# A convolution in Winograd-like form with four filtered positions: filter weights by accumulating transfers, shared rows copied, norm sums over eight rows, and the last reordering moved into the next chunk

## The chip, the cores and the metric

The kernel runs on one core of one Trainium2 chip. The metric is the device time of one execution in microseconds; the median of several runs counts. In the text, PE is TensorE, DVE is VectorE, ACT is ScalarE, POOL is GpSimd and SP is SyncE; PEld is PE's loading of weights.

## The reference, cut to what matters

Four layers work on x of shape (4, 256, 56, 56) in float32. Each normalises by groups of eight channels (`_gn`), applies a block and adds the result to its input.

```python
x = x + _L0_conv_ref(_gn(x), ...)   # involution, 7x7 window, weights computed from x
x = x + _L1_conv_ref(_gn(x), ...)   # residual block of two 3x3 convolutions
x = x + _L2_conv_ref(_gn(x), ...)   # involution with batch norms
x = x + _L3_conv_ref(_gn(x), ...)   # gates from the spectrum's mean and the channel mean

def _L1_conv_ref(x, w1, g1, b1, rm1, rv1, w2, g2, b2, rm2, rv2):
    h = _conv3x3(x, w1, stride=1)
    h = _bn(h, g1, b1, rm1, rv1)
    h = jax.nn.relu(h)
    h = _conv3x3(h, w2, stride=1)
    h = _bn(h, g2, b2, rm2, rv2)
    return jax.nn.relu(x + h)

def _gn(v, G=32, eps=1e-5):
    g = v.reshape(B_, G, C_ // G, H_, W_)
    m = jnp.mean(g, axis=(2, 3, 4), keepdims=True)
    s = jnp.var(g, axis=(2, 3, 4), keepdims=True)
    return ((g - m) / jnp.sqrt(s + eps)).reshape(v.shape)
```

The change concerns the second layer, `_L1_conv_ref`, alone.

## The kernel before, in words

`involution_layer` does layers 0 and 2 (the fourth layer's gates run inside its second call), and `conv_layer` the two 3x3 convolutions between them. Channels are two blocks of 128 partitions (`NB` = 2).

**The form.** Along a row, groups of four output pixels are computed from six transformed input values (positions k = 0 to 5) instead of by twelve products. `phases` normalises the loaded rows into four interleaved planes `ph1` on ACT (L1331). `transform` makes six position planes v from them in nine DVE instructions (L1355 to L1369); `input1` does so for the first convolution, `input2` for the second, out of `ph2`, in which the first leaves its result. For each position PE multiplies v with position weights (`unfiltered`, L1413: two input blocks times three row taps). In the first convolution, from chunk 1 on, the positions 1 to 4 (`K2`) are filtered along the rows too: `columns` (L1392 to L1395, DVE) combines rows of v, PE does four products (L1451) into an `inner` and an `outer` pair of PSUM banks, ACT copies one (L1461), and DVE joins them (L1465, L1466, L1468).

**The weights.** `u1_sb` and `u2_sb` hold six positions for each of two input blocks and three taps. `row_weights` loads positions 0 and 5 and computes positions 1 to 4 from the three filter columns on DVE, six instructions for each block (L1246 to L1255); `edge_weights` multiplies positions 0 and 5 on ACT (L1261). `column_weights` (DVE) and `filter_weights` (ACT, L1267) make the filtered weights of the first convolution.

**The order.** An image is three chunks of rows, so there are twelve chunks in each convolution: `C1_ROWS` is 20, 18, 18 rows and `C2_ROWS` is 16, 20, 20. The order on all engines is written out by hand: (1, 0), then (1, i), (2, i - 1) in turn, then (2, 11). Side work is put into twelve slots `after[0]` to `after[11]` of each chunk: `after[2 * n]` runs at the first half of the n-th position, `after[2 * n + 1]` behind it. `in_order` then ties each engine to this program order. In `conv1` the copy L1461 of a filtered position stands ahead of `after[2 * n]`.

**The end of a chunk.** `conv2` scales the residual (L1515, ACT), joins it with the result (L1527, DVE), reorders it by a relu on ACT (L1535), adds the layer's input by an accumulating DMA (L1536, POOL) and stores it (L1537, POOL). This is done for each half of the channels (`co` = 0, 1), at the chunk's end. In the next conv2 chunk `stats` takes the sums for the following norm, one instruction for each four rows (L1544). `conv1`'s last two outputs (L1430) are left in `tail1` and run in the following conv2 chunk; in the one place where a conv1 chunk follows another, chunk 1 after chunk 0, they run at its start.

**Buffers.** `mm_ps` has four tiles of two PSUM banks, which all the products take in turn, those of `norm_steps` too. `norm_steps` is a generator that advances at `after[5]` and `after[11]` and keeps its tile from the product (L217, L228) to the step in which DVE reads it (L220, L148). `y_tile(0)` to `y_tile(4)` and `y_tile(5)` are scratch for results. `v` has two buffers in turn.

Of the kernel before, what the change touches and what calls it, by code (L numbers as in the profile page):

```python
# [56 lines left out]
C2_ROWS = [(0, 16), (16, 36), (36, 56)]  # L57
ST_ROWS = 4

# [12 lines left out]
def net_kernel(  # L72
# [1109 lines left out]
    def conv_layer(xin, xout, st, ahead):  # L1182
        with ExitStack() as es:
# [44 lines left out]

            def row_weights(u, wc, raw=None):

                ws = []
                for ci in range(NB):
                    w = wc[ci * P : (ci + 1) * P].rearrange("c (y x) n -> c y x n", y=3)
                    nc.sync.dma_start(u[:, ci, :, 0, :], w[:, :, 0, :])
                    nc.sync.dma_start(u[:, ci, :, 5, :], w[:, :, 2, :])
                    us = [u[:, ci, :, k, :] for k in range(WPOS)]
                    if raw is None:
                        w1 = new_xr()[:, : 3 * C].rearrange("p (y n) -> p y n", y=3)
                        nc.scalar.dma_start(w1, w[:, :, 1, :])
                        ws.append((us[0], w1, us[5], *us[1:5]))  # L1240
                    else:
                        r = raw[ci][:, : 9 * C].rearrange("p (y x n) -> p x y n", y=3, x=3)
                        ws.append((r[:, 0], r[:, 1], r[:, 2], *us[1:5]))
                yield
                for w0, w1, w2, u1, u2, u3, u4 in ws:
                    tt(u2, w0, w2, ALU.add)  # L1246
                    tt(u1, u2, w1, ALU.add)
                    yield
                for w0, w1, w2, u1, u2, u3, u4 in ws:
                    tt(u2, u2, w1, ALU.subtract)  # L1250
                yield
                for w0, w1, w2, u1, u2, u3, u4 in ws:
                    stt(u4, w2, 4.0, w0, ALU.mult, ALU.add)
                    stt(u3, w1, 2.0, u4, ALU.mult, ALU.add)
                    stt(u4, w1, -2.0, u4, ALU.mult, ALU.add)  # L1255
                    yield

            def edge_weights(u, ci):

                for k, by in ((0, 6.0), (5, 24.0)):  # L1260
                    nc.scalar.mul(u[:, ci, :, k, :], u[:, ci, :, k, :], by)  # L1261

# [6 lines left out]
            def column_weights(ci, k0, k1):  # L1269

                w0, w1, w2 = (u1_sb[:, ci, y, k0:k1, :] for y in range(3))
                x = ux_sb[:, ci, k0 - 1 : k1 - 1, :]
                s = y_tile(3)[:, : (k1 - k0) * C].rearrange("p (k n) -> p k n", n=C)
                tt(s, w0, w2, ALU.add)
                tt(x, s, w1, ALU.subtract)
                tt(w1, s, w1, ALU.add)
# [38 lines left out]
            def phases(i):  # L1315

                y0, y1, lo, hi = rows1(i)
                n, r0 = y1 - y0 + 2, lo - (y0 - 1)
                rstd, shift = norms[1][i // 3]
                if y0 == 0:  # L1320
                    nc.vector.memset(ph1[:, :, 0], 0.0)
                if y1 == H:
                    nc.vector.memset(ph1[:, :, n - 1], 0.0)
                for ci in range(NB):
                    at = ci * (CV_ROWS + 2) * W
                    xr = room["rows"][:, at : at + (hi - lo) * W].rearrange("p (r t j) -> p j r t", t=WT, j=4)
                    for j in range(4):
                        q, t0 = (j + 1) % 4, (j + 1) // 4
                        dst = ph1[:, PL[q], r0 : r0 + hi - lo, ci, t0 : t0 + WT]
                        s, t = rstd[:, ci : ci + 1], shift[:, ci : ci + 1]  # L1330
                        nc.scalar.activation(dst, xr[:, j], AF.Identity, bias=t, scale=s)  # L1331
                        yield

            def transform(v, ph, y0, n):

                rows = ph[:, :, y0 : y0 + n].rearrange("p j r c t -> p j (r c) t")
                at, size = rows[:, 0:1], ph.shape[2] * NB * (WT + 1)
# [33 lines left out]

            def new_v(key):
                v_of[key] = work.tile([P, WPOS, (CV_ROWS + 2) * NB, WT], F32, name="v")
                return v_of[key]

            def input1(i):
                y0, y1, _, _ = rows1(i)
                n = y1 - y0 + 2
                yield from transform(new_v((1, i)), ph1, 0, n)

            def input2(i):
                y0, y1 = C2_ROWS[i % 3]
                yield from transform(new_v((2, i)), ph2, y0, y1 - y0 + 2)

# [32 lines left out]
            def conv1(i, after, tail):  # L1417
# [4 lines left out]
                a, t, b, s, q = (y_tile(k)[:, : NB * n * WT] for k in (0, 1, 2, 5, 4))  # L1422
                home = {1: q, 2: s, 3: t, 4: s, 0: s}

# [14 lines left out]
                for n_s, k in enumerate(KS):  # L1439
# [41 lines left out]
                    if k == 2:  # L1481
                        tt(full(a), full(q), got, ALU.add)
                        tt(full(q), got, full(q), ALU.subtract)
                    elif k == 4:
# [14 lines left out]
            def conv2(i, after, sums, tail):  # L1499
# [23 lines left out]
                def joined(co):  # L1523
# [7 lines left out]
                    if i == n_chunks - 1:  # L1531
                        stt(xj, rj, 0.0, xj, ALU.max, ALU.add)
                        nc.sync.dma_start(xout[bb][co][:, at], x)
                    else:
                        nc.scalar.activation(xj, rj, AF.Relu)  # L1535
                        nc.gpsimd.dma_start(x, xin[bb][co][:, at], accum_op=ALU.add)  # L1536
                        nc.gpsimd.dma_start(xout[bb][co][:, at], x)  # L1537

                def stats(co, ks):

                    x = xr_of[i, co]
                    for k in ks:
                        at = (k * ST_ROWS - y0) * W
                        nc.vector.bn_stats(sums[co][:, k, :], x[:, at : at + ST_ROWS * W])  # L1544

# [36 lines left out]

                ks = list(range(y0 // ST_ROWS, y1 // ST_ROWS))
                tail += [lambda co=co, part=part: stats(co, part) for co in range(NB) for part in (ks[:2], ks[2:])]


# [10 lines left out]
            order.append((2, n_chunks - 1))  # L1597
            late_v = None
            sums_of = {}


            since = mark()
            weights1, weights2 = row_weights(u1_sb, wc1, (room["h"], room["v2"])), row_weights(u2_sb, wc2)
            next(weights1)
# [24 lines left out]
            for s, (conv, i) in enumerate(order):  # L1629
                after = [[] for _ in range(12)]  # L1630
                for g in slow:
                    after[5].append(step(g))
                    after[11].append(step(g))
                nxt = order[s + 1] if s + 1 < len(order) else None
                if conv == 1:
                    run_all(tail1)

                    if nxt[0] == 2:
                        j = nxt[1]
                        late_v = input2(j)  # L1640
                        place(after, late_v, (1, 1, 3, 5, 8, 10))
                        if j == 0:
                            place(after, weights2, (3, 5, 7, 9, 11))
                        if i + 1 < n_chunks:
# [3 lines left out]
                    else:  # L1648
                        j = nxt[1]
                        place(after, phases(j), [k // 2 for k in range(8)])  # L1650
                        after[3].append(lambda: load_rows(j + 1, xin))
                        place(after, input1(j), [4 + k // 2 for k in range(9)])
                        for ci in range(NB):
                            after[2 + ci].append(lambda ci=ci: edge_weights(u1_sb, ci))
                            after[4 + ci].append(lambda ci=ci: column_weights(ci, 1, 3))
# [3 lines left out]
                        for ci in range(NB):  # L1659
                            after[9 + ci].append(lambda ci=ci: column_weights(ci, 3, 5))  # L1660
                            after[10 + ci].append(lambda ci=ci: filter_weights(ci, 3, 5))
                        after[11].append(step(weights2))
                    conv1(i, after, tail1)
                else:
                    if i % 3 == 0:
                        sums_of[i // 3] = [
                            new_sums(H // ST_ROWS, work, 4)
                            if i // 3 < B - 1
                            else small.tile([P, H // ST_ROWS, 6], F32, name=f"st_c{co}", bufs=1)
                            for co in range(NB)  # L1670
# [3 lines left out]
                    tail1 = []  # L1674
                    if i == 0:
                        for ci in range(NB):
                            after[ci].append(lambda ci=ci: edge_weights(u2_sb, ci))
                    if late_v is not None:
                        place(after, late_v, (0, 0, 1))
                        late_v = None  # L1680
                    stats_at, loads_at = ((1, 2, 3, 4), (2, 4)) if i < n_chunks - 1 else ((3, 4, 6, 7), (4, 7))
                    for at, f in zip(stats_at, tail2):
                        after[at].append(f)
                    tail2 = []
# [20 lines left out]

            return tail2, sums_of[B - 1]

# [77 lines left out]
```

## Time and profile before

| | |
|---|---|
| median of 3 runs | 1776.24 us (1775.5 to 1786.09) |
| the profiled execution | 1783.97 us |
| its span in the profile | 1782.2 us |
| PE busy | 1704.1 us (96%) |
| PE weight loads | 1504.1 us (84%) |
| DVE busy | 1333.3 us (75%) |
| ACT busy | 898.5 us (50%) |
| POOL busy | 397.1 us (22%) |

The profile shows one execution; its times count from the start of its span. A group of instructions is named by line, engine and tiles, with its count, its busy time and the idle time before it with what ended it. PEclk is the share of full clock that PE was granted. The convolutions' matmuls run from 520.3 to 1228.8 us, and a conv1 chunk begins there with L1451 rows and ends with L1413 rows.

### The profile page before, as it was taken

The numbers are of one execution on the slowest core, as the hardware profiler recorded it, in microseconds if no ns is written. First come the engines' busy times: TensorE is split into PE (matmuls) and PEld (weight loads), VectorE is DVE, ScalarE is ACT, GpSimd is POOL, SyncE is SP. The second block draws the span as 40 slices with busy tenths as digits, with TensorE's granted clock in tenths as the row PEclk, the third lists the DMA queues.
The fourth block names the chain that finished last, engine by engine and source line by source line (L and its number), as shares of the span: only waits on it lengthen the run. The fifth ranks groups of instructions, "written<-read, shape, count | busy, mean of one in ns | idle before, by whom it ended". The sixth has DMA issues, their size and how long they took to land.

```text
span 1782.2 us, 55628 instructions
## 1 busy us (share of the span) xinstructions
PE 1704.1 (96%) x24128; PEld 1504.1 (84%) x24128; DVE 1333.3 (75%) x2457; ACT 898.5 (50%) x1909; POOL 397.1 (22%) x591
## 2 busy tenths in 40 slices
PE   6999999999989999999999999998999999999898
PEld 4988988889978988898889889986888888888786
DVE  2777787767779887788778787865877677678675
ACT  2555556555554424432343334223667567577555
POOL 2224322333320000000000000001000554562572
PEclk9999999999999999999999999999999999999996
DMA  2445443633652123331333132233445666665643
GB/s 86 136 151 179 134 149 132 197 107 128 205 178 92 45 70 90 93 79 42 84 92 89 39 90 52 63 126 108 143 139 167 191 201 196 211 210 159 193 147 114
DMA packets 71074, 227.45 MB, mean 128 GB/s; under 512 B 13141, under 2 KB 20830, under 8 KB 67118
## 3 DMA queue, kind: packets, MB, share of 16 engines
q1 hardware_dynamic: 55038, 160.97, 28.6%
q0 software_dynamic: 13952, 60.87, 12.2%
q8 instruction: 190, 3.11, 0.7%
q10 hardware_dynamic: 1840, 2.05, 0.4%
q14 instruction: 54, 0.44, 0.1%
HBM read 88.00 MB, written 49.15 MB: 77 GB/s over the span
## 4 chain that ended last, share of the span: by engine, by line
PE 70%; DVE 17%; ACT 4%; issue 4%; DMA 3%; POOL 1%; SPq 1%; ACTq 0%; DVEq 0%; POOLq 0%
PE mm L1413 25%; PE ps L634 14%; PE ps L592 14%; PE mm L1451 7%; DVE kt L610 5%; PE ps L406 3%; DVE un L654 3%; DMA xw<-xw 2%; PE ps L468 2%; DVE st L1104 1%; DVE st L359 1%; ACT xs L1535 1%; ACT hp L487 1%; PE ps L717 1%; PE ps L946 1%
## 5 line engine op out<-in xcount | busy, mean ns | idle before, releaser
L1413 PE MATMUL mm<-v,u_sb 128*128 128x280 f32 (+2 forms) x2400 | 533.8, 384 | 1.2 <-DVE v L1367 1.2
L1413 PEld LDWEIGHTS mm<-v,u_sb 128*128 128x128 f32 x2400 | 452.4, 189 | 77.6 <-PE mm L1413 1.9
L634 PE MATMUL ps<-kt,xw 126*32 126x48 f32 (+1 forms) x12544 | 382.8, 236 | 31.2 <-issue 23.0
L634 PEld LDWEIGHTS ps<-kt,xw 126*32 126x32 f32 (+1 forms) x12544 | 343.2, 122 | 77.8 <-issue 55.5
L592 PE MATMUL ps<-hp,z_sb 64*126 64x133 f32 x6144 | 383.8, 279 | 7.3 <-DVE kt L610 4.4
L592 PEld LDWEIGHTS ps<-hp,z_sb 64*126 64x126 f32 x6144 | 365.0, 186 | 22.5 <-DVE kt L610 6.2
L610 DVE TENSOR_TENSOR kt<-ps,zb_sb 126x798 f32<-126x798 f32 x352 | 333.0, 980 | 60.2 <-PE ps L592 48.7
L603 ACT ACTIVATE kt<-ps,zb_sb 126x133 f32<-126x133 f32 x960 | 280.3, 441 | 105.8 <-PE ps L592 105.8
L654 DVE SCALAR_TENSOR_TENSOR un<-ps,s,un 128x240 f32<-128x240 f32 x224 | 102.4, 457 | 88.7 <-ACT un L649 84.5
L654 DVE SCALAR_TENSOR_TENSOR un<-ps,par_sb,un 128x240 f32<-128x240 f32 x224 | 97.9, 456 | 85.2 <-ACT un L647 81.2
L1451 PE MATMUL mm<-xs,u_sb 128*128 128x126 f32 (+1 forms) x1056 | 133.7, 280 | 7.7 <-DVE hp L1466 6.8
L1451 PEld LDWEIGHTS mm<-xs,u_sb 128*128 128x128 f32 x1056 | 127.9, 194 | 9.7 <-ACT ph L1331 8.3
L418 ACT COPY xw<-ps 126x896 f32<-126x896 f32 x112 | 101.3, 906 | 42.3 <-PE ps L406 22.4
L659 POOL TENSOR_TENSOR xs<-un,xs 128x240 f32<-128x240 f32 x112 | 72.2, 665 | 219.8 <-DVE un L654 219.8
L406 PE MATMUL ps<-ident_sb,strip_sb 128*126 128x128 f32 x784 | 112.7, 285 | 6.3 <-issue 3.0
L1536 POOL DMA_DIRECT2D xs<-x x22 | 19.7, 897 | 441.4 <-ACT xs L1535 441.4
L149 POOL TENSOR_TENSOR norm_sb<-norm_sb,mhalf 128x1 f32<-128x1 f32 x32 | 19.3, 605 | 432.6 <-DVE norm_sb L148 432.6
L647 ACT ACTIVATE un<-ps,par_sb 128x240 f32<-128x240 f32 x112 | 50.1, 448 | 122.5 <-PE ps L634 112.1
L649 ACT ACTIVATE un<-ps,bn_t,s 128x240 f32<-128x240 f32 x112 | 60.1, 537 | 98.5 <-PE ps L634 90.9
L1535 ACT ACTIVATE xs<-res 128x1120 f32<-128x1120 f32 (+1 forms) x22 | 45.9, 2088 | 126.6 <-DVE res L1527 126.6
L406 PEld LDWEIGHTS ps<-ident_sb,strip_sb 128*126 128x126 f32 x784 | 85.7, 143 | 17.4 <-POOL strip_sb L391 4.1
L1331 ACT ACTIVATE ph<-xs,norm_sb 128x294 f32<-128x294 f32 (+2 forms) x96 | 80.8, 896 | 8.8 <-DMA xs<-x 7.1
(253 smaller groups left out, 1819.8 us busy)
## 6 DMA issues: line engine op xcount, KB each, us to landing
xw<-xw SPq DMA_DIRECT2D x224, 252.0 KB
xw<-xw SPq DMA_DIRECT2D x224, 126.0 KB
xs<-x SPq DMA_DIRECT2D x24, 560.0 KB
x<-xs POOLq DMA_DIRECT2D x8, 1568.0 KB, 8.2
xs<-x SPq DMA_DIRECT2D x8, 1568.0 KB
xs<-in_x_dram SPq DMA_DIRECT2D x6, 1568.0 KB
x<-xs SPq DMA_DIRECT2D x6, 1568.0 KB
gx<-x POOLq DMA_DIRECT2D x42, 224.0 KB, 5.3
```

Of the source, the lines that this page charges most:

```text
L406: nc.tensor.transpose(ps[:Q, k * P : (k + 1) * P], flat[:, k * Q : (k + 1) * Q], ident_sb)
L418: nc.scalar.copy(xw[:, :NSB, :], ps[:Q, : NSB * P].rearrange("q (n c) -> q n c", n=NSB))
L592: nc.tensor.matmul(ps[:Q, i, k * NT : (k + 1) * NT], z_sb[i * R : (i + 1) * R, cb * GB // 2 + gp, z0 : z0 + Q], hp[i * R : (i + 1) * R, py ...
L603: nc.scalar.activation(kt[:, g0 + i, pb, :, k], ps[:Q, i, k * NT : (k + 1) * NT], AF.Identity, bias=zb_sb[:, cb * GB + g0 + i, p0 + k : p0 ...
L610: nc.vector.tensor_tensor(kt[:, g0 : g0 + 2, pb], ps[:Q, :, : PB * NT].rearrange("q i (k t) -> q i t k", k=PB), zb_sb[:, cb * GB + g0 : cb ...
L634: nc.tensor.matmul(v[m * j : m * j + m, i, :, k * TP : (k + 1) * TP], xw[:, window(ty), m * j : m * j + m], kt[:, ng * j : ng * j + ng, :, ...
L654: nc.vector.scalar_tensor_tensor(part, o[e], s, part, ALU.mult, ALU.add)
L659: nc.gpsimd.tensor_tensor(dst, u, dst, ALU.add)
L1331: nc.scalar.activation(dst, xr[:, j], AF.Identity, bias=t, scale=s)
L1413: nc.tensor.matmul(ps, *position(u, v, ci, dy, k, co, n), start=(j == 0), stop=(j == NB * 3 - 1))
L1451: nc.tensor.matmul(ps[:, bank, co * m : (co + 1) * m], u[ci][:, co * P : (co + 1) * P], v2[:, e, : n // 2, ci * WT : (ci + 1) * WT], start ...
L1535: nc.scalar.activation(xj, rj, AF.Relu)
```

## The change

1. `row_weights` stays for the first convolution. For the second, `summed_weights` loads the raw filter columns straight into the position planes, multiplies three of them on ACT, and adds the other columns by accumulating DMAs from POOL, 18 of 384 KB in nine pairs; a last step on ACT multiplies positions 0 and 5. The steps are placed in the slots of chunks (1, 0) and (1, 1).
2. `transform` takes `known`: where a chunk follows another of the same image, the two rows that both use are copied on ACT from the place in v where the chunk before left them, and the DVE instructions cover two rows fewer. `phases` leaves these rows out too. The two v buffers are named, and used in the same turn.
3. `ST_ROWS` is 8 instead of 4: a half image of sums is 8 instructions (2, 3 and 3 by chunk) instead of 14. They stand around the load of the residual that overwrites their rows.
4. In `conv2` the relu, the accumulating DMA and the store of the second half go into `late_x` and run at `after[0]` of the next chunk, that is, behind the first copy of conv1. `tail1` of chunk 0 goes to `after[0]` of chunk 1 likewise, and from chunk 1 on the first filtered result has `y_tile(3)` as its place.

```diff
-ST_ROWS = 4
+ST_ROWS = 8
+ST_PIECES = [-(-(y1 - y0) // ST_ROWS) for y0, y1 in C2_ROWS]
...
+            def summed_weights(u, wc):
+
+                cis = range(NB)
+                w = [wc[ci * P : (ci + 1) * P].rearrange("c (y x) n -> c x y n", y=3) for ci in cis]
+                us = [[u[:, ci, :, k, :] for k in range(WPOS)] for ci in cis]
+                w1 = [new_xr()[:, : 3 * C].rearrange("p (y n) -> p y n", y=3) for ci in cis]
+                for ci in cis:
+                    nc.sync.dma_start(w1[ci], w[ci][:, 1])
+                    nc.sync.dma_start(us[ci][5], w[ci][:, 2])
+                    for k in (0, 1, 3):
+                        nc.sync.dma_start(us[ci][k], w[ci][:, 0])
+                yield
+                for ci in cis:
+                    nc.scalar.mul(us[ci][2], w1[ci], -1.0)
+                    nc.scalar.mul(us[ci][4], w1[ci], -2.0)
+                    nc.scalar.mul(us[ci][5], us[ci][5], 4.0)
+                    yield
+                for k, x in ((1, 1), (2, 0), (1, 2), (2, 2), (3, 1), (4, 0), (3, 1), (4, None), (3, None)):
+                    for ci in cis:
+                        by = us[ci][5] if x is None else w[ci][:, x]
+                        nc.gpsimd.dma_start(us[ci][k], by, accum_op=ALU.add)
+                    yield
+                for ci in cis:
+                    for k in (0, 5):
+                        nc.scalar.mul(us[ci][k], us[ci][k], 6.0)
+                yield
...
-                    xr = room["rows"][:, at : at + (hi - lo) * W].rearrange("p (r t j) -> p j r t", t=WT, j=4)
+                    xr = room["rows"][:, at + known * W : at + (hi - lo) * W].rearrange("p (r t j) -> p j r t", t=WT, j=4)
...
-            def transform(v, ph, y0, n):
-
+            def transform(v, ph, y0, n, known):
+
+                if known is not None:
+                    old, m = known
+                    nc.scalar.copy(
+                        v[:, :, : 2 * NB].rearrange("p k r t -> p k (r t)"),
+                        old[:, :, m * NB : (m + 2) * NB].rearrange("p k r t -> p k (r t)"),
+                    )
+                    v, y0, n = v[:, :, 2 * NB :], y0 + 2, n - 2
...
+                v = v_of[1, i] = v_sb[min(i, 1)]
+                p0, p1 = C1_ROWS[i % 3 - 1]
+                known = (v_of[1, i - 1], p1 - p0) if i % 3 else None
+                yield from transform(v, ph1, 0, y1 - y0 + 2, known)
...
-                home = {1: q, 2: s, 3: t, 4: s, 0: s}
+                first = y_tile(3)[:, : NB * n * WT] if i else q
+                home = {1: first, 2: s, 3: t, 4: s, 0: s}
...
-                        nc.scalar.activation(xj, rj, AF.Relu)
-                        nc.gpsimd.dma_start(x, xin[bb][co][:, at], accum_op=ALU.add)
-                        nc.gpsimd.dma_start(xout[bb][co][:, at], x)
...
+                        late_x.append(lambda: added(x, xj, rj, co, at))
+                        if co == 0:
+                            run_all(late_x)
+
+                def added(x, xj, rj, co, at):
+
+                    nc.scalar.activation(xj, rj, AF.Relu)
+                    nc.gpsimd.dma_start(x, xin[bb][co][:, at], accum_op=ALU.add)
+                    nc.gpsimd.dma_start(xout[bb][co][:, at], x)
+
+                def stats(co, k):
+
+                    r0, r1 = k * ST_ROWS, min(n, (k + 1) * ST_ROWS)
+                    at = sum(ST_PIECES[: i % 3]) + k
+                    nc.vector.bn_stats(sums[co][:, at, :], xr_of[i, co][:, r0 * W : r1 * W])
...
+                after[0] += late_x
+                late_x.clear()
                 if conv == 1:
-                    run_all(tail1)
+                    after[0] += tail1
+                    tail1 = []
...
-                        place(after, late_v, (1, 1, 3, 5, 8, 10))
+                        place(after, late_v, (1, 1, 3, 5, 8))
                         if j == 0:
-                            place(after, weights2, (3, 5, 7, 9, 11))
+                            place(after, weights2, (0, 1, 2, 11))
...
+                        place(after, weights2, (0, 4, 5, 5, 6, 7, 8, 9, 10))
                         place(after, input1(j), [4 + k // 2 for k in range(9)])
...
-                    if i == 0:
-                        for ci in range(NB):
-                            after[ci].append(lambda ci=ci: edge_weights(u2_sb, ci))
                     if late_v is not None:
-                        place(after, late_v, (0, 0, 1))
+                        place(after, late_v, (0, 0, 1, 1))
...
-                    stats_at, loads_at = ((1, 2, 3, 4), (2, 4)) if i < n_chunks - 1 else ((3, 4, 6, 7), (4, 7))
-                    for at, f in zip(stats_at, tail2):
-                        after[at].append(f)
+                    loads_at = (2, 4) if i < n_chunks - 1 else (4, 7)
+                    for at, fs in zip(loads_at, tail2):
+                        for k, f in enumerate(fs):
+                            after[at - (k == 0)].append(f)
```

## The prediction

> **What bounds the kernel now.** I read the page first, then the busy time by stage, then TensorE's (PE's) waits inside the convolution stage, and last the order of time around each PE stall. The change touches only that stage.
>
> ```profile
> span 1782.2 us, 55628 instructions
> PE 1704.1 (96%) x24128; PEld 1504.1 (84%) x24128; DVE 1333.3 (75%) x2457; ACT 898.5 (50%) x1909; POOL 397.1 (22%) x591
> ```
>
> ```profile
> 520.30:1228.80 708.50, 699.66 (x3837) 620.62 (x3835) 569.16 (x980) 260.74 (x320) 37.16 (x51) 1.00 0.28 78
> ```
>
> The stage from 520.3 to 1228.8 us has PE busy 699.7 of 708.5 us, VectorE (DVE) 569 (80%), ScalarE (ACT) 261. PE is the bound, and the change removes no matmul. What DVE or ACT gain is worth only the PE stalls that it ends. The list of PE's waits has three entries there:
>
> ```profile
> PE mm L1451 <- DVE hp L1466: 6.8, 4, 2.2
> PE mm L1413 <- DVE v L1367: 1.2, 2, 0.6
> ```
>
> (the third, ACT ph L1331, is 0.4 us). A stall can cost more than its idle time, so I measured the filtered part of each conv1 chunk in PE's timeline, from its first L1451 row to the next L1413 row. An undisturbed chunk of 18 rows takes 14.29 us (732.97 to 747.26), one of 20 rows 15.25 (672.44 to 687.69). Four chunks are longer: chunk 1 19.23 (555.32 to 574.55, loss 4.9), chunk 2 15.27 (loss 1.0), chunk 6 19.71 (843.97 to 863.68, loss 4.5), chunk 9 18.25 (1020.12 to 1038.37, loss 3.0). In chunks 1 and 6 the stall is followed by slow matmuls; the table by stage has PEclk 0.91 in both and 1.00 in chunk 9:
>
> ```profile
> 844.00:863.60 19.60, 17.38 (x129) 17.02 (x130) 13.89 (x26) 10.06 (x13) 3.64 (x6) 0.91 0.60 146
> 1020.10:1038.30 18.20, 15.77 (x130) 15.41 (x130) 13.86 (x26) 10.10 (x13) 3.72 (x6) 1.00 0.64 157
> ```
>
> With the two L1367 stalls (0.63 at 532.46 in chunk 0, 0.55 at 594.77), all that can be won in the stage is 4.9 + 1.0 + 4.5 + 3.0 + 1.2 = 14.6 us.
>
> Why chunks 1, 6 and 9? There are four two-bank PSUM tiles, and a filtered position needs two. In these chunks `norm_steps` holds one or two tiles as well: it computes a mean just before the chunk (L217 at 555.18, two L228 at 843.61) and DVE reads it only at `after[5]` (573.25, 860.40). PE then has two or three tiles and follows the DVE closely. Around chunk 6:
>
> ```profile
> 846.74 2.21 ACT L1535 ACTIVATE xs<-res 128x1120 f32<-128x1120 f32 x1 [1.45 <-DVE res L1527]
> 848.76 0.43 ACT L1461 COPY xs<-mm 128x280 f32<-128x280 f32 x1
> 849.22 0.45 DVE L1465 TENSOR_TENSOR hp<-xs,mm 128x280 f32<-128x280 f32 x1 [1.86 <-ACT xs L1461]
> 850.17 1.86 PE L1451 MATMUL mm<-xs,u_sb 128*128 128x140 f32 x8 [2.14 <-DVE hp L1466]
> ```
>
> The reader is to see the chain: the previous conv2 chunk's reordering relu (L1535) stands on ACT ahead of the copy (L1461) that DVE needs to free PE's tile. In chunk 1 the same copy comes at 562.15, behind four L1430 outputs (2.15 us) that follow the last filter weights (ended 560.2).
>
> **What the Trainium skill says.** "TensorE: Matmul & The Clock Gate", part 1, says that an idle window of about 3.4 us puts PE to half clock, with windows that run freely. The trace agrees in kind: idle of 2.1 to 2.2 us was followed by slow matmuls in chunks 1 and 6 but not in 9. "DMA: Bandwidth & Descriptors", section on the anatomy of one DMA, gives 2.0 us plus bytes/436e3 per transfer from GpSimd (POOL): 2.9 us, an estimate, for 393 KB. The trace's accumulating transfers are dearer: 5.7 us median to landing for 560 KB rows (L1536), 0.91 us on POOL to issue. The same page says descriptor generation is "small, variable"; no row here has a POOL transfer of 384 pieces.
>
> **The change part by part.**
>
> *Relu of the second half after the first copy (`late_x`).* The same instructions, moved past one copy. Chunk 6, with the durations above: inner tile done at 845.9, ACT free at 845.3, copy 846.1 to 846.5. DVE is then the later one: L1527 ends 846.7, L1392 847.4, L1465 and L1466 848.2. PE's first two tiles are done at 848.0: stall 0.2 instead of 2.1, and no half clock. What is late next: ACT does relu (to 849.0), the new row copy (0.5), a phase (0.9), then the second copy, 850.4 to 850.8. DVE does L1355 twice, L1394, L1395, L1392, L1465, L1466, in all about 3.7 us after 849.5, so the third inner tile is free at 853.2 against PE ready at 852.1: stall 1.1. Chunk 6 ends 2.8 us earlier than now, chunk 9 (where nothing slowed) 1.4. The accumulating and storing DMAs of that half (L1536, L1537) start about as before or up to 0.3 us later; their readers come over 10 us on. In the other chunks four tiles are free and nothing waits.
>
> *Outputs of chunk 0 after the copy (`tail1`), and weights of conv2.* Chunk 1: copy at 560.2, L1466 ends 561.3, PE (out of work at 561.2) stalls 0.2. Then outputs to 562.7, a phase to 563.5, second copy 563.9; DVE waits for the outputs until 562.7 before L1355 and frees the second inner tile at 566.4, PE ready at 565.2: stall 1.2. End about 572.0 instead of 574.55: gain 2.5. L1246 to L1255 for u2, twelve DVE instructions of 0.95, 11.4 us, leave DVE between 570 and 593. The 0.55 stall at 594.77 goes, since L1367 stood behind five of them. The 0.63 at 532.46 stays: it is behind u1's weights, which still go through DVE.
>
> *What replaces them.* SP: ten loads of 393 KB instead of four, ahead of the next `load_rows`. The four u1 loads and row loads ran at about 350 GB/s, so 3.9 MB take 11 to 12 us, landed by 538; rows(1) are ahead of them in SP's queue, rows(2) wait for phases until 533 anyway. ACT: six multiplications (L1261's 0.78 each, 4.7 us) between 534 and 541.5, where it has idle gaps before the L1267 and L1430 rows: nothing. The four edge multiplications only move. POOL: 18 accumulating transfers in nine pairs; of one plane each waits for the one before it. The first pair waits for its load, the second for ACT (540). If 0.9 us to issue and 5.7 to land hold, u1 and u2 are whole by 552 and the last pair, third in its plane, lands at about 566. conv2 chunk 0 asks for position 1 at 584.9, position 3 at 594.3. Cover: 28 us. Bounds: nothing, if that holds; if POOL gives one transfer at a time, 540 + 16 x 5.7 = 631, PE waits 37 us. I take nothing, since the waits in the program are only between transfers of the same plane, and keep 37 for a rival. Also behind the last pair on ACT: the multiplication by 6 at `after[11]` of chunk 1 (584), with outputs and the next copy behind it.
>
> *Shared rows copied.* 16 transforms of 9 DVE instructions lose 2 of 20 or 22 rows: single ones 0.06 us (0.80 to 0.74), double ones 0.115 (1.435 to 1.32), 0.74 us each, 12 us of DVE in all; phases lose 0.1 each on 64. ACT gets 16 copies of 128 x 336, by L1461 (0.37 for 252) about 0.45 to 0.5. The DVE's first step waits for the copy. In conv2 ACT is idle then. In conv1 the copy stands behind the relu, and DVE waits about 0.5 us; with four tiles PE has more than 2 us of slack there. Cost on the path: nothing, except in chunks 6 and 9, where it is in the sum.
>
> *Sums over eight rows.* Per half image 8 instructions for 14, then a shorter aggregate: about 1 to 2 us of DVE per image, under PE. *Buffers by name, first result in tile 3:* the same places and order, nothing.
>
> Chunk 2 loses its 1.0 to the same L1535 order (copy at 619.10); gain 0.7.
>
> Sum: 2.5 + 0.55 + 0.7 + 2.8 + 1.4 = 8.0 us. The profiled execution took 1783.97 us (span 1782.2 and 1.8 around it), which would be 1776.0. It is 7.7 us over the median of the runs shown; I carry the difference over: 1776.24 - 8.0 = 1768.2.
>
> **The rivals.** (a) All stalls go but the one at 532.46 (the DVE, 12% lighter, frees tiles before PE asks, though a norm holds some): 14.6 - 0.6 = 14.0, 1762.2. For it: every loss starts with a late copy. Against: with two tiles DVE's own chain is 4.5 to 5 us a position against 3.8 of PE. (b) Nothing: DVE now waits for ACT's row copies, and what the copy of tile 1 gains is lost at tile 2 (relu, row copy and phase are 3.6 us of ACT in a position of 3.6 to 3.8); 1776. (c) Slower: accumulating transfers land one at a time. They decide from the point where the sixteen after 540 need over 3.4 us each, 594.3; at 5.7 us PE idles 37 us in conv2 chunk 0: 1768.2 + 37 = 1805. For it: before, POOL never has two in flight. Against: the waits in the program. (d) That the change doesn't do what it says: the instruction order shows relu and outputs behind the first copy, and DVE's weight rows gone; not a case of weight.
>
> **How the numbers follow.** The forecast, 4 to 12 us less, has 0.64; (a) 0.12; (b) 0.15; (c) 0.09, part of it with a small wait. The range 1760 to 1781 holds the first three and their spread, the runs differing by 10 us among themselves, and leaves (c) out. One per cent, 17.8 us, is about what a measurement of this kernel can tell from no change: faster by more needs more than all stalls (0.05), slower by more is (c) (0.08), the rest is within.
>
> **What would show it.** Right: chunks 1, 6 and 9 at about 16.7, 16.9 and 16.9 us, PEclk 1.00 in them, no L1367 stall near 594, all of u2 accumulated before 575. Wrong: PE or ACT waiting for a POOL transfer between 560 and 630; a PE wait in a chunk that has none now; POOL rows of over 1.5 us each for the 18 transfers; or the stalls gone while the span stays, which would put the loss outside the stage.

## The result and the profile after

The kernel after took 1770.25 us at the median of 11 runs (1765.71 to 1774.86), the kernel before 1779.32 us at the median of 11 runs beside it (1775.5 to 1786.09). The ratio is 0.994, 95% interval 0.9923 to 0.9957. The forecast was 1768.2 us with a range of 1760 to 1781. It called a gain of 8.0 us; the ratio is one of 10.7 us (7.7 to 13.7), and the medians differ by 9.1.

The page of the profiled execution (1767.96 us), its first lines, busy time and share by engine:

```profile
span 1765.9 us, 55633 instructions
PE 1696.1 (96%) x24128; PEld 1497.1 (85%) x24128; DVE 1306.7 (74%) x2397; ACT 908.3 (51%) x1931; POOL 416.9 (24%) x609
```

DVE is busy 26.6 us less, and PE has the same matmuls. The table by stage gives, for each stretch, its length, busy time of PE, PEld, DVE, ACT and POOL, the granted clock, and the DMA's share and GB/s. First the convolution stage, then the filtered parts of chunks 1, 6 and 9:

```profile
520.30:1220.00 699.70, 696.92 (x3839) 618.01 (x3839) 545.28 (x925) 268.98 (x342) 58.47 (x69) 1.00 0.36 92
556.80:572.70 15.90, 14.87 (x132) 14.55 (x131) 14.70 (x33) 11.44 (x21) 7.88 (x7) 1.00 1.22 212
840.40:857.00 16.60, 15.70 (x129) 15.34 (x129) 13.47 (x26) 10.33 (x14) 3.59 (x5) 1.00 0.70 161
1013.40:1030.00 16.60, 15.75 (x129) 15.39 (x129) 13.45 (x26) 10.34 (x14) 3.58 (x5) 1.00 0.71 163
```

Chunk 6 took 19.6 us with PE busy 17.4 at clock 0.91 before; it takes 16.6 with PE busy 15.7 at 1.00 now. So part of the 3 us was idle time, and part was matmuls that had been slow after it. PE's waits in the stage were 6.8 us on L1466 and 1.2 on L1367. This is what the list of PE's waits holds of it now (us in total, times, longest):

```profile
PE mm L1485 <- DVE xs L1500: 2.2, 3, 0.8
PE mm L1485 <- DVE hp L1500: 0.6, 3, 0.2
```

(L1485 and L1500 are L1451 and L1466 of before; the listing above keeps the lines of before.) The timeline around chunk 6 shows the new order, start and length in us, and in brackets the idle time before with what ended it:

```profile
842.54 0.39 ACT L1495 COPY xs<-mm 128x280 f32<-128x280 f32 x1 [0.84 <-PE mm L1485]
843.15 2.27 ACT L1575 ACTIVATE xs<-res 128x1120 f32<-128x1120 f32 x1 [0.22 <-DVE res L1561]
844.62 1.19 PE L1485 MATMUL mm<-xs,u_sb 128*128 128x140 f32 x8 [0.22 <-DVE hp L1500]
845.20 0.51 ACT L1361 COPY v<-v 128x336 f32<-128x336 f32 x1
845.73 1.39 DVE L1385 SCALAR_TENSOR_TENSOR v<-ph 128x560 f32<-128x560 f32 x2 [0.42 <-ACT v L1361]
849.36 1.19 PE L1485 MATMUL mm<-xs,u_sb 128*128 128x140 f32 x8 [0.69 <-DVE xs L1500]
```

The copy (L1495) now comes ahead of the relu (L1575). PE's stall at the first inner tile is 0.22 us where it was 2.14. A second stall of 0.69 us comes at the next position, with relu, row copy (L1361) and phase between the two copies on ACT.

All later comparisons are made in one unit: the length of the convolution stage and of its parts in the profiled execution, read from PE's rows. A chunk's filtered part runs from its first filtered row to its next unfiltered one. "Head" is the unfiltered work of chunk 0; "conv2 chunk 0" is the unfiltered stretch between chunks 1 and 2. An undisturbed filtered part takes 14.29 us (18 rows) or 15.25 us (20 rows); chunks 3 and 4, which nothing disturbs, agree within 0.01 us in all twelve kernels here.

| kernel | stage | chunk 1 | chunk 2 | chunk 6 | chunk 9 | conv2 chunk 0 | head |
|---|---|---|---|---|---|---|---|
| before | 708.50 | 19.23 | 15.27 | 19.71 | 18.24 | 38.45 | 34.97 |
| after | 697.80 | 15.91 | 14.29 | 16.72 | 16.67 | 37.67 | 34.10 |
| difference | 10.70 | 3.32 | 0.98 | 2.99 | 1.57 | 0.78 | 0.87 |

The six parts are 10.5 of the 10.7 us; chunk 7 has the other 0.2. The spans differ by 16.3 us. The rest of that is not in the change: the stage starts 2.3 us later after, and what follows it took 7.9 us less (545.4 against 553.3), with the same code but for the last sums of the norm. Over the profiled executions of all kernels here that last part lies between 543.4 and 558.8 us.

### The profile page after: what moved, and what is told of

It reads as the page before. It is cut to its first block, busy times and chain, and to the rows that moved or that the text cites. A ratio compares the mean times of both kernels' runs of the same rounds, so it can differ in the third digit from the quotient of the medians.

```text
span 1765.9 us, 55633 instructions
## 1 busy us (share of the span) xinstructions
PE 1696.1 (96%) x24128; PEld 1497.1 (85%) x24128; DVE 1306.7 (74%) x2397; ACT 908.3 (51%) x1931; POOL 416.9 (24%) x609
## 4 chain that ended last, share of the span: by engine, by line
PE 73%; DVE 12%; DMA 5%; ACT 4%; issue 3%; SPq 1%; POOL 1%; ACTq 0%; DVEq 0%; POOLq 0%
PE mm L1446 27%; PE ps L635 15%; PE ps L593 14%; PE mm L1485 8%; DVE kt L611 5%; PE ps L407 3%; DMA xw<-xw 3%; DVE un L655 3%; PE ps L469 2%; DMA u_sb<-in_wc_dram 1%; DVE st L1105 1%; ACT hp L488 1%; SPq L425 1%; PE ps L718 1%; PE ps L947 1%
## 5 line engine op out<-in xcount | busy, mean ns | idle before, releaser
L1485 PE MATMUL mm<-xs,u_sb 128*128 128x126 f32 (+1 forms) x1056 | 130.4, 277 | 2.8 <-DVE xs L1500 2.2
L1485 PEld LDWEIGHTS mm<-xs,u_sb 128*128 128x128 f32 x1056 | 125.2, 191 | 4.2 <-ACT ph L1354 1.7
L1576 POOL DMA_DIRECT2D xs<-x x22 | 19.6, 889 | 444.2 <-ACT xs L1575 444.2
L1575 ACT ACTIVATE xs<-res 128x1120 f32<-128x1120 f32 (+1 forms) x22 | 46.3, 2106 | 117.1 <-DVE res L1561 117.1
L150 POOL TENSOR_TENSOR norm_sb<-norm_sb,mhalf 128x1 f32<-128x1 f32 x32 | 19.1, 599 | 356.4 <-DVE norm_sb L149 356.4
```

The source lines that it names most:

```text
L1485: nc.tensor.matmul(ps[:, bank, co * m : (co + 1) * m], u[ci][:, co * P : (co + 1) * P], v2[:, e, : n // 2, ci * WT : (ci + 1) * WT], start ...
```

## The experiments

Two questions were open. Which of the change's parts brings the time, and is the cause of the stalls the late copy on ACT, or the PSUM tiles that `norm_steps` holds? And how close are the accumulating transfers to being the bound? In all kernels but one (`a_longw`, the last) the whole computation is kept.

### Is it the held tiles? `b_norm` and `a_norm`

The steps of `norm_steps` run in conv2 chunks only, so that no tile is held across a filtered part. `b_norm` is this edit on the kernel before, `a_norm` on the kernel after:

```diff
-                for g in slow:
-                    after[5].append(step(g))
-                    after[11].append(step(g))
+                for g in slow if conv == 2 else ():
+                    for k in (0, 3, 5, 8, 10, 11):
+                        after[k].append(step(g))
```

> The kernel before with one edit: norm_steps advances only in conv2 chunks, at after[0], 3, 5, 8, 10 and 11, so that no PSUM tile is held while a conv1 chunk runs. Theory (the held tile makes the stalls): chunks 1, 6 and 9 fall from 19.2, 19.7 and 18.2 us to about 14.5, 15.3 and 15.3, PEclk 1.00 in them; 10 to 12 us less in all, although ACT's first copy is as late as before. Rival (the late copy alone makes them, the tile is incidental): chunks 1, 6 and 9 stay within 1 us of what they are, and the time within 2 us.

> The changed kernel with the same edit to norm_steps. Theory (what is left in chunks 1, 6 and 9, 1.6, 1.5 and 1.4 us, is the held tile): they fall to 14.3 to 14.5, 15.3 and 15.3 us, 4 to 4.5 us less than the changed kernel in all, some 13 to 15 less than before. Rival (what is left is DVE's own chain of work, or the new waits for ACT's row copies): they stay at 15.9, 16.7 and 16.7.

`b_norm` took 1781.93 us against 1784.63, ratio 0.9998 (0.9982 to 1.0015), stage 707.84: no gain. It doesn't settle the question, since the parts moved both ways: chunk 1 19.23 to 17.53, chunk 6 19.71 to 17.23 and chunk 9 18.24 to 17.34, but chunk 2 15.27 to 16.37 and conv2 chunk 0 38.45 to 41.77. `a_norm` took 1771.63 us against 1784.63, ratio 0.9926 (0.9899 to 0.9953), stage 699.19, which is 1.4 us over after. Chunk 1 fell to its floor (15.91 to 14.29), and chunk 2 rose from 14.29 to 16.38. The timeline of `a_norm` around chunk 6 shows why:

```profile
846.67 0.56 POOL L1577 DMA_DIRECT2D x<-xs  x1 [5.25 <-DMA xs<-x]
847.24 1.09 POOL L150 TENSOR_TENSOR norm_sb<-norm_sb,mhalf 128x1 f32<-128x1 f32 x2
847.85 0.16 DVE L233 SCALAR_TENSOR_TENSOR norm_sb<-gm,norm_sb 128x1 f32<-128x1 f32 x1 [3.72 <-POOL norm_sb L150]
850.03 1.19 PE L1485 MATMUL mm<-xs,u_sb 128*128 128x140 f32 x8 [1.22 <-DVE hp L1500]
```

My slots were badly chosen. The norm's small power (L150) is queued on POOL behind the store L1577, which waits 5.25 us for its accumulating DMA. The norm's shift (L233) waits on DVE for the power, and everything that DVE does for PE stands behind it for 3.72 us. One stall had been traded for another. The test had to be made again with other slots.

### The same with the norm finished early: `a_norm2` and `b_norm2`

```diff
-                    for k in (0, 3, 5, 8, 10, 11):
+                    for k in (0, 2, 3, 5, 6, 7, 7):
```

> The changed kernel with norm_steps advanced in conv2 chunks alone, at after[0], 2, 3, 5, 6, 7 and 7, so that POOL's power stands ahead of the accumulating DMAs of the chunk's end (in a_norm DVE's L233 waited 3.7 to 4.3 us for it behind a store) and no tile is held in conv1. Theory: chunks 1, 2, 6 and 9 at 14.29, 14.29, 15.25 and 15.25 us, none of the conv1 chunks with a PE wait over 0.3; the stage 693 to 694 us against 697.8, some 4 us less than the changed kernel. Rival (DVE's chain of 4.5 us a position limits the chunk whatever the tiles): 6 and 9 stay over 16.2.

> The kernel before with norm_steps at after[0], 2, 3, 5, 6, 7 and 7 of conv2 chunks (as in a_norm2) and nothing else: four tiles free in every conv1 chunk, the first copy on ACT as late as before. Theory (a late copy stalls PE only where tiles are held): chunks 2, 6 and 9 at 14.3, 15.3 and 15.3 us, chunk 1 17 to 18 (there ACT and DVE are behind by the weights as well), the stage 698 to 701 us against 708.5. Rival (the late copy stalls PE by itself): 6 and 9 over 17.

`a_norm2` took 1763.72 us against 1786.56, ratio 0.9873 (0.9842 to 0.9905). Its stage is 693.56 us, 4.2 under after. In the table by stage, chunks 1, 6 and 9 and the whole stage:

```profile
554.30:568.60 14.30, 14.30 (x129) 14.26 (x128) 13.21 (x27) 11.28 (x21) 6.54 (x6) 1.00 1.24 200
836.60:851.80 15.20, 15.20 (x129) 15.20 (x128) 13.46 (x24) 10.67 (x14) 2.45 (x4) 1.00 0.75 173
1008.20:1023.40 15.20, 15.20 (x129) 15.20 (x128) 13.46 (x24) 10.68 (x14) 2.45 (x4) 1.00 0.76 173
520.00:1220.00 700.00, 699.46 (x3866) 619.01 (x3864) 548.15 (x931) 271.18 (x344) 63.64 (x75) 1.00 0.37 92
```

PE's busy time equals the length of each stretch: the three chunks are at their floor, and PE idles nowhere in them. All stalls that after still has there were those of held tiles. The edit also takes the norm's small DVE steps out of these chunks, but in before the only ones in chunk 6 (two, 0.22 us together) stand at 860.40, ten us behind the stall. The program says the same: the filtered products of chunk 1 use three tiles in turn in before and after (0, 2, 1), those of chunks 6 and 9 only two; in `a_norm2` they use all four.

`b_norm2` took 1781.19 us against 1785.36, ratio 0.997 (0.9952 to 0.9989), stage 701.42, just over the 698 to 701 that I expected. It answers what `b_norm` left open. Its chunks 6 and 9 in the table by stage:

```profile
844.20:859.40 15.20, 15.20 (x129) 15.20 (x128) 12.13 (x21) 10.42 (x13) 2.46 (x4) 1.00 0.74 174
1016.00:1031.20 15.20, 15.20 (x129) 15.20 (x128) 12.14 (x21) 10.41 (x13) 2.28 (x4) 1.00 0.68 150
```

They are at the floor too, 4.5 and 3.0 us under before, with the copy just as late as before. The timeline of ACT in that kernel, chunk 6:

```profile
847.34 2.22 ACT L1535 ACTIVATE xs<-res 128x1120 f32<-128x1120 f32 x1 [1.45 <-DVE res L1527]
849.36 0.43 ACT L1461 COPY xs<-mm 128x280 f32<-128x280 f32 x1
```

So in chunks 6 and 9 a copy this late does not stop PE by itself: with four tiles it has two positions in hand. There the stall needs both, the late copy and a held tile. Either can be taken away; the change takes the first.

That is no rule for a copy that is later still. Chunk 1 of `b_norm2` is 17.53 us, though its program uses all four tiles in turn. Its first copy starts at 561.82, 7.0 us after the chunk's first product (5.2 in chunk 6), behind the four outputs L1430, and PE waits 0.9 us. At the chunk's end PE waits 1.5 us more for DVE, where L1465 stands behind two instructions of the second convolution's weights (L1246 and L1247, 1.9 us).

The gain of `b_norm2` was partly lost in conv2 chunk 0, 41.76 us for 38.45. There the norm's steps now meet the weights of the second convolution on DVE, and PE waits for the norm's own sums: the aggregate L214 starts at 591.73, directly behind the weights' L1253 to L1255. From its list of PE's waits, first the two of chunk 1, then those of conv2 chunk 0:

```profile
PE mm L1413 <- DVE hp L1466: 1.5, 1, 1.5
PE mm L1451 <- DVE hp L1466: 0.9, 1, 0.9
PE mm L217 <- DVE mv L214: 2.6, 1, 2.6
PE mm L228 <- DVE d L225: 0.7, 1, 0.7
```

### The moved reordering: `b_moves`, `a_nomoves` and `b_moves_norm2`

`b_moves` is the kernel before with `late_x` and `tail1` moved and the first filtered result in `y_tile(3)`, as in the fourth point of the change, and nothing else. `a_nomoves` is the kernel after without the two moves:

```diff
-                        if co == 0:
-                            run_all(late_x)
+                        run_all(late_x)
...
-                    after[0] += tail1
-                    tail1 = []
+                    run_all(tail1)
```

> The kernel before with the moves alone: late_x, tail1 behind the first copy and the first result in tile 3; weights of conv2 on DVE, no row copies, sums over four rows. Theory (the late copy is what the change ends): chunk 6 about 17, chunk 9 about 16.9, chunk 2 about 14.3 us, chunk 1 16 to 17; the 0.55 us stall in conv2 chunk 0 stays; 7 to 9 us less than before. Rival (the 12% lighter DVE does it): chunks 6 and 9 stay near 19.7 and 18.2, under 3 us less.

> The changed kernel with the relu, accumulation and store of the second half at the end of its conv2 chunk again and chunk 0's outputs ahead of chunk 1. Theory: chunks 6 and 9 at 18.5 to 20, chunk 1 at 17.5 to 19, chunk 2 up to 15.3; the stage 704 to 707 us, that is 6 to 9 more than the changed kernel. Rival (with the lighter DVE the order doesn't matter): under 700.

`b_moves` took 1777.67 us against 1784.63, ratio 0.9962 (0.9942 to 0.9981), stage 699.70: 8.8 us less by these few lines, of which 0.9 lie in the head, that the moves do not touch. Chunks 6 and 9 are 16.29 each, even 0.4 shorter than in after. Chunk 1 stays at 17.82. What is left on PE:

```profile
PE mm L1452 <- DVE hp L1467: 2.0, 4, 1.4
PE mm L1452 <- DVE xs L1467: 1.4, 3, 0.8
PE mm L1413 <- DVE v L1367: 0.6, 1, 0.6
```

The wait for L1367 is that behind the weights on DVE, untouched by the moves. So is the longest on L1467, 1.4 us in chunk 1, which stands behind L1246 and L1247.

`a_nomoves` took 1776.55 us against 1786.56, ratio 0.9943 (0.9924 to 0.9963), stage 702.61: 4.8 over after, less than I expected: chunk 1 is 17.26, chunk 2 stays at 14.29, and chunks 6 and 9 rise to 18.14 and not to 19.7. Its longest wait is 2.2 us, as in before, but no slow matmuls follow it (the granted clock is 1.00 in all three chunks):

```profile
PE mm L1485 <- DVE hp L1500: 6.5, 3, 2.2
```

Last, both remedies on the kernel before, moves and early norm, without any other part of the change:

> The same with the moves of the relu and of chunk 0's outputs added; conv2's weights on DVE, no row copies, sums over four rows. Theory (tiles and order are enough in chunks 6 and 9; the weights on DVE still cost chunk 1 and the stall near 592): chunks 6 and 9 at 15.3, chunk 1 15 to 17.5, stage 695 to 698 us, 2 to 4 more than a_norm2's 693.6. Rival (tiles and order are all): stage under 694.5.

It took 1778.71 us against 1785.36, ratio 0.9963 (0.9945 to 0.9981), stage 699.47. I missed this, having expected 695 to 698: chunks 2, 6 and 9 are at their floor and chunk 1 is 16.10, with a wait of 1.4 us on L1467, yet conv2 chunk 0 is 41.76 again, with the same waits as in `b_norm2`. The early norm pays in full only where the weights are off DVE; that is what `a_norm2` has and this kernel has not.

### The weights on DVE again: `a_dve`

The kernel after, with `row_weights` for the second convolution as in before, its steps and the edge multiplications in their old slots:

```diff
-            weights1, weights2 = row_weights(u1_sb, wc1, (room["h"], room["v2"])), summed_weights(u2_sb, wc2)
+            weights1, weights2 = row_weights(u1_sb, wc1, (room["h"], room["v2"])), row_weights(u2_sb, wc2)
...
-                            place(after, weights2, (0, 1, 2, 11))
+                            place(after, weights2, (3, 5, 7, 9, 11))
...
-                        place(after, weights2, (0, 4, 5, 5, 6, 7, 8, 9, 10))
```

> The changed kernel with conv2's weights made by twelve DVE instructions again, everything else as changed. Theory (accumulating transfers buy only the 0.55 us stall and some of chunk 1): the same as the changed kernel in chunks 6 and 9 (16.7), the stall of about 0.5 us near 592 back, chunk 1 up by under 1 us: 0.5 to 1.5 us more than the changed kernel. Rival (the weights are a main part): 3 us or more.

It took 1776.32 us against 1784.63, ratio 0.9964 (0.9944 to 0.9985). Its stage is 701.46, 3.7 over after: 1.7 in chunk 1 and 2.0 in conv2 chunk 0. The other theory's "3 us or more" held, not mine. PE's row after the weights:

```profile
592.69 18.40 PE L1424 MATMUL mm<-v,u_sb 128*128 128x224 f32 x96 [1.73 <-DVE v L1375]
```

This stall was 0.55 us in before. Here it is 1.2 us larger, since the step of the transform that PE waits for (L1375, L1367 of before) stands one slot later than it did: on DVE two steps of the next transform (L1363, 1.27 us) now come ahead of it, which in before came behind it. In part, then, `a_dve` prices the weights in after's order and not in before's; without these 1.2 us, 2.5 would be left, between the two theories.

### The row copies: `a_norows`

```diff
-                n, r0, known = y1 - y0 + 2, lo - (y0 - 1), 2 if i % 3 else 0
+                n, r0, known = y1 - y0 + 2, lo - (y0 - 1), 0
...
-                known = (v_of[1, i - 1], p1 - p0) if i % 3 else None
+                known = None
...
-                known = (v_of[2, i - 1], p1 - p0) if i % 3 else None
+                known = None
```

> The changed kernel without the shared rows: every chunk normalises and transforms all its rows again, no copies on ACT. Theory (the row copies are on the path where two tiles are left): chunks 6 and 9 about 16.3 instead of 16.7 us, chunk 1 about the same, the stage within 1 us of the changed kernel's 697.8. Rival (the 12 us of DVE that they save are worth something): 2 us or more longer.

It took 1765.84 us against 1786.56, ratio 0.9899 (0.9865 to 0.9934), stage 697.44 against 697.80. The row copies take work from DVE and bring nothing. In chunks 6 and 9 they cost 0.4 us each (16.32 and 16.31 without them), because DVE waits for a copy that stands behind the relu on ACT; chunk 1 gets 0.24 shorter with them.

### How close are the accumulating transfers? `a_longw`

The kernel after with the last two pairs of accumulating transfers made three times, eight transfers more; positions 3 and 4 of the second convolution's weights are therefore other values:

```diff
-                for k, x in ((1, 1), (2, 0), (1, 2), (2, 2), (3, 1), (4, 0), (3, 1), (4, None), (3, None)):
+                for k, x in ((1, 1), (2, 0), (1, 2), (2, 2), (3, 1), (4, 0), (3, 1)) + 3 * ((4, None), (3, None)):
...
-                            place(after, weights2, (0, 1, 2, 11))
+                            place(after, weights2, (0, 1, 2, 3, 4, 5, 6, 11))
```

> The changed kernel with the last two pairs of accumulating transfers made three times (eight transfers more; the weights of positions 3 and 4 get their last column three times, so conv2's values are changed). Theory from the profile after (the last pair landed at 585, 13 us after its issue, and PE asks for position 3 at 592): two rounds of about 13 us more end near 611, PE waits 15 to 20 us in conv2 chunk 0. Rival (the prediction's 5.7 us a transfer and 28 us of cover): no PE wait.

It took 1796.22 us in its one run. Conv2 chunk 0 grew from 37.67 to 54.58 us, and the chain can be read from four rows of the timeline, in order of time:

```profile
601.75 1.57 ACT L1278 ACTIVATE u_sb<-u_sb 128x768 f32<-128x768 f32 x2 [21.45 <-DMA u_sb<-u_sb]
605.57 0.45 ACT L1361 COPY v<-v 128x336 f32<-128x336 f32 x1
606.05 1.28 DVE L1385 SCALAR_TENSOR_TENSOR v<-ph 128x504 f32<-128x504 f32 x2 [17.68 <-ACT v L1361]
608.02 20.92 PE L1446 MATMUL mm<-v,u_sb 128*128 128x224 f32 x96 [14.15 <-DVE v L1397]
```

ACT waits for the last transfers at the multiplication by 6 (L1278). Behind it on ACT stands the next chunk's row copy (L1361). DVE waits for that, and PE for DVE. Two parts of the change make this path together: the weights put a DMA wait on ACT, and the row copy puts DVE behind ACT. The row copy is not the whole of it, though. PE asked for position 3 at 593.9, and the last transfer, which belongs to that position, landed at 603.8. Without the row copy PE would still have had to wait some 10 us for the weights themselves (an estimate from these two times; no run tried it). Of the 16.9 us, 14.15 are this wait; the matmuls after it are slower too (96 in 20.92 us, against 18.40 for the same row of `a_dve` above). The danger that rival (c) named is real, only not reached: 26 transfers cost 17 us, 18 cost PE nothing.

## Why the prediction was right, point by point

**What bounds, and why chunks 1, 6 and 9.** Right, and now shown. PE's stalls were all there was to win: the forecast counted 14.6 us of loss, and `a_norm2`, without a stall in the stage, is 14.9 under before. Their place was that of the held tiles: released early, they leave chunks 1, 6 and 9 at the floor in `a_norm2`, and 2, 6 and 9 in `b_norm2`. The forecast named two conditions, the late copy and the held tile, and in chunks 6 and 9 the runs show that the stall needs both. In chunk 1 it doesn't: with four tiles it stays at 17.53 in `b_norm2`, by a copy that is later still and by the weights on DVE.

**The relu behind the first copy.** Right in size. For chunk 6 the sum gave 16.9 us with stalls of 0.2 and 1.1; it is 16.72 with 0.22 and 0.69. For chunk 9 it gave 16.9; it is 16.67. Gains of 2.8 and 1.4 were called, 3.0 and 1.6 came. The clock is 1.00 in all three chunks, as called. The Trainium skill's page "TensorE: Matmul & The Clock Gate", part 1, asks for idle of about 3.4 us; in this case slow matmuls followed idle of 2.1 to 2.2 us in two of three places of before and in none of the same three in `a_nomoves`, and a stall of 0.7 us slowed nothing. What decides it these runs don't show. So about 1.5 of chunk 6's 3.0 us, the slow stretch after its stall (19.71 us against 18.24 in chunk 9, which stalled alike), and about as much in chunk 1 (24 matmuls in 4.54 us, against 2.91 after the same idle of 2.24 us in `a_nomoves`) may be luck of the profiled execution.

**Outputs of chunk 0 behind the copy, and chunk 1.** Right in kind, short in size: 2.5 us called, 3.3 measured (15.91 us, not 16.7). `b_moves` and `a_dve`, which have the weights of the second convolution on DVE, both leave chunk 1 near 17.7. So of the 3.3 us 1.4 are the moves (19.23 to 17.82, a slow stretch of before in it), 1.7 the DVE time that the weights gave up (17.58 to 15.91), and the last 0.2 the row copies (`a_norows`, 16.15). I had given that DVE time only the 0.55 us stall behind it. This term is the one mis-sized part on the gain's side: by `a_dve` it is worth 3.7 us of stage in after's order, 1.2 of them of that order's own making.

**The stall of 0.63 us in chunk 0 that "stays".** It is gone: the head is 34.10 us for 34.97. That isn't explained. `b_moves`, whose code there is that of before, has 34.10 too, and the heads of the other kernels lie between 33.96 and 34.83, so I count it neither for the change nor against it.

**Shared rows, sums over eight rows, buffers.** The row copies are as called: no gain, and a small cost in chunks 6 and 9 only. The sums over eight rows were not tried by themselves.

**The accumulating transfers.** The conclusion held, that they cost PE nothing, but the step behind it failed, and that it held is in part luck. I took 0.9 us to issue, 5.7 to land, the last pair landed at 566, and 28 us of cover. One of my own signs of a wrong forecast, "ACT waiting for a POOL transfer between 560 and 630", came true, and one of a right one, "all of u2 accumulated before 575", did not. The source line's view of L1274 in the kernel after, least, median and greatest in ns, then landing in us:

```profile
L1274 POOL DMA_DIRECT2D u_sb<-in_wc_dram x14: 1129/1206/2851, 534.6 to 564.2; - x14
L1274 POOL DMA_DIRECT2D u_sb<-u_sb x4: 1258/1269/1272, 565.9 to 571.9; - x4
DMA to landing us min/median/max: 7.5/9.5/13.1
```

and who waited for the last ones on ACT:

```profile
582.39 1.58 ACT L1278 ACTIVATE u_sb<-u_sb 128x768 f32<-128x768 f32 x2 [3.60 <-DMA u_sb<-u_sb]
585.12 0.84 ACT L1278 ACTIVATE u_sb<-u_sb 128x768 f32<-128x768 f32 x1 [1.15 <-DMA u_sb<-u_sb]
```

The last transfer landed at about 585.1, 19 us later than I said. By `a_longw`'s path, ACT then has the row copy done at 587.3 and DVE the next position (L1397) at 589.2; PE asks for it at 592.4. The cover is 3.2 us, not 28. By the measure of the forecast's rival (c), the seventeen transfers issued from 540.2 on took 2.6 us each (to 585.1), where 3.4 would decide. `a_longw` agrees: counted from the start of its conv2 chunk 0, which comes 1.5 us later, its last transfer landed 17.2 us later (603.8 against 585.1), and PE stood for 14.15, so 3.1 us were covered. What I left out is that the engines have a rate, not only a delay: 17.2 us for eight more transfers are 2.15 us each, and 393 KB in that time are 183 GB/s. I could have known: in the packet records of before, the 3,584-byte packets of L1536 already took 291 ns at the median, which is 197 GB/s over sixteen engines.

**The rivals.** (a), that all but one of the stalls go, is what `a_norm2` does, and it takes one thing more than the change: the tiles. The DVE that (a) called 12% lighter is 26.6 us lighter, under 5% of its 569 us in the stage. (b), that the gain is lost at the second tile, holds for 0.7 us of it. (c) did not occur: several transfers were in flight at once, each landing after 9.5 us at the median while one was done every 2.6. But 3 us were to spare instead of 28.

`a_norm2` is the version to keep. Beside `a_norows`, whose stage is within 0.4 us of after's and which ran against the same runs of before, its ratio is lower by 0.0026, or 4.6 us, and its stage by 3.9. The intervals of the two ratios overlap (six runs each), so the stage is the firmer of the two figures.

## What to carry to other kernels

When PE stalls in some rounds of a loop and not in others, ask first which buffers are held in just those rounds: here a sum of one column, kept in a PSUM tile until a later slot, took away a quarter of the buffering of much larger products in chunk 1, and half of it in chunks 6 and 9. A chain of DMAs is to be sized by its bytes over the measured rate of that kind of packet, besides the delay of one. And a wait that is moved to an engine with free time becomes a wait of all that stands behind it there: here ACT behind a DMA, DVE behind ACT, and PE behind DVE.

## What the runs showed of the hardware that was not expected

Accumulating transfers run at about half the rate of plain loads of the same pieces. The DMA view of the kernel after, packets of 1 KB: first plain loads of weight columns (6 us from 528), then the accumulating transfers (8 us from 556), when no other data queue was moving anything:

```profile
DMA packets 2165, 2.15 MB, mean 358 GB/s; under 512 B 88, under 2 KB 2163, under 8 KB 2163
```

```profile
DMA packets 1576, 1.56 MB, mean 196 GB/s; under 512 B 63, under 2 KB 1575, under 8 KB 1575
```

All sixteen engines are busy in both stretches. A packet that accumulates takes about 81 ns of an engine (16 x 8 us / 1575) against 44 (16 x 6 us / 2163). The stretches differ in the issuing queue as well, SP's against POOL's. But in the packet records of before, POOL's plain packets of 3,584 bytes (after 1380 us) took 140 ns at the median, and its accumulating ones 291, so the queue is not the reason there. The Trainium skill's page "DMA: Bandwidth & Descriptors", in its section on the anatomy of one DMA, gives 2.0 us plus bytes/436e3, an estimate of 2.9 us for each of these; the median here is 9.5 us, with several under way at once on one set of engines. POOL's share of it, 1.13 to 1.27 us for 384 pieces (the rows of up to 2.85 us stand in a line of five that took 5.90 us, 1.18 each), is 0.2 to 0.4 us over the 0.91 us that it took for the accumulating transfers of 128 pieces.
